# A four-layer graph network on one core: first node states interleaved by four, segment flags moved into the first attention pass, edge parts one supertile earlier

## The chip, the core and the metric

The kernel runs on one core of one Trainium2 chip. A core has five engines with a queue of instructions each: TensorE (PE in the profile, its weight loads PEld), VectorE (DVE), ScalarE (ACT), GpSimd (POOL) and SyncE (SP), and 16 DMA engines. [...] SP only issues DMAs here; GpSimd issues the indirect ones (gathers and scatters). The metric is the device time of one execution in microseconds (us).

## The reference

The graph has 5000 nodes and 80000 edges, sorted by destination; node states and edge attributes have 128 features. Four layers follow each other, each on the normalised and rectified state, each added back to it:

```python
h = relu(layernorm(x)); x = x + L0(h, edges, edge_attr_128)   # three steps of attention (GAT) + GRU
h = relu(layernorm(x)); x = x + L1(h, edges)                  # GIN: a sum of neighbours, two matmuls, batch norm
h = relu(layernorm(x)); x = x + L2(h, edges, edge_attr_4)     # four steps of a gated graph network
h = relu(layernorm(x)); x = x + L3(h, edges)                  # graph transformer
```

Layer 0, the one of the change, computes in each of its three steps, with H = 4 heads of 32:

```python
q = x[dst] @ wq.T + bq
k = (x[src] + edge_attr) @ wk.T + bk          # v likewise
a = softmax over the edges of one dst of sum(q * k, per head) / sqrt(32)
out[dst] = sum over its edges of a * v
```

followed by a projection, layer norms, a two-layer MLP and a GRU cell on the nodes. The part `edge_attr @ wk.T` (and wv) is the same in all three steps.

## The kernel before, in words

**Tiling.** Nodes are held transposed, features on the 128 partitions, in 10 groups (`NG`) of 512 columns (`GW`); the last group is partly empty. Edges are cut into 157 supertiles (`NSUP`) of four tiles of 128 edges. Because the edges are sorted, the destinations of a supertile lie in a window of 128 nodes that moves by 32 a supertile.

**Order of the work.** The Tile layer allocates the buffers, sets the semaphores and orders the instructions of each engine; inside `tc.manual_schedule()` the order is that of the program text. Around the change:

1. `tile_gnn` (L1844) loads the destinations and checks that the sorted form fits; `sorted_graph` (L782) then loads small weights and constants.
2. `index_edges` (L869 to 912) loads sources and the four edge type scores, finds each edge's type on DVE, transposes the indices on TensorE into `srcx`, `typx`, `dneg`, and stores two tables, `key_t` (L905, L909) and `dl_t` (L912), through SP.
3. The weights of layer 0 are loaded (L1532, 1.18 MB). Then come the *first states* (L1536 to 1562): for each group the rows of x are loaded (L1549, through SP, two buffers), transposed (L1555), copied from PSUM (L1557), stored, normalised and rectified by `Chain.norm` (L1063 to 1092), and turned into rows of k, v, q by `qkv_tables` (L1127 to 1141), which stores them in the tables `kv_t` and `q_t`. `norm` is a chain: matmul L1066 (centre), Square on ACT L1069, four small matmuls L1074 (variance), Sqrt L1077, reciprocal and a diagonal on DVE L1079 and L1080, matmul L1083 (spread over partitions), copy L1085, product L1088. `qkv_tables` is four times a matmul L1132 and an addition on DVE L1135. Generators write these chains: each `yield` ends a step. Here `alone()` runs a chain to its end before the next group begins.
4. `segments` (L914 to 925) makes, for each of the 20 chunks (`NCH`) of eight supertiles, flags that tell where a destination's run of edges begins and ends. Per chunk: one load of destinations, two DVE instructions, one store into `seg_t`, with two buffers.
5. `gat_pass` (L1265 to 1410) runs three times, in manual order. One loop step `s` does the following, in this order: two zero blocks of the count table for later layers (`zero_counts`, first pass only, 120 in all); a step of `place_counts` (first pass only), which ends in 185 scatters on GpSimd; `prefetch(s + 4)`: in the first pass the raw edges `e` (L1281), then the query rows `qw` and destinations `dl`, all from SP, and four gathers of kv rows by GpSimd (L865); the sums of supertile `s - 12` (L1206); the addition of the edge part to the gathered kv (L1377, DVE); `edge_part(s + 1)` (first pass); products with the queries (L1383) and the values with their edge part (L1385); `expand(s + 1)`, which spreads the queries over the edges on TensorE (L1247); the scores (L1391); `flip_edges(s + 2)` (first pass); the weighted values (L1260) and the one-hot of supertile `s - 11` (`one_hot`, L1212 to 1220, five ACT instructions); `flip(s + 2)` for the queries (L1240, DVE). Between these, four calls of `go()` each advance one step of a softmax chain and of a node chain (`gat_node`).

`flip_edges` transposes the raw edges on TensorE (L1297) and copies them on ACT (L1299). `edge_part` multiplies them with the weights of k and v (L1308), copies the result on ACT (L1310) into `ekv` and stores it (L1311) for passes two and three, which load it instead. Each lives in a dictionary under its supertile's number:

```python
            if here:
                n, kv, e = tiles_of(s), kvs.pop(s), ekvs.pop(s)
                V.tensor_add(kv[:, :n, :D], kv[:, :n, :D], e[:, :n, :D])
            if first and 0 <= s + 1 < NSUP:
                edge_part(s + 1)
```

Of the kernel before, what the change touches and what calls it, by code (L numbers as in the profile page):

```python
# [47 lines left out]
P = 128  # L48
# [3 lines left out]
G = 4  # L52
# [702 lines left out]
def tiles_of(s):  # L755
    return min(G, NT - s * G)
# [25 lines left out]
def sorted_graph(ctx: ExitStack, tc, x, src, ea, ea4, wpack, rpack, out, dpad, dnat):  # L782
# [86 lines left out]
    def index_edges():  # L869
        with tc.tile_pool(name="ix", bufs=1) as ix, \  # L870
                tc.tile_pool(name="ip", bufs=2, space=PSUM) as ip:
            n = NT // TI
            src_i = ix.tile([n, TI * P], I32, name="src_i")
            Y.dma_start(src_i, src.rearrange("(p c) -> p c", p=n))
            e4 = ix.tile([n, TI * P, 4], F32, name="e4")
            Y.dma_start(e4, ea4.rearrange("(p c) f -> p c f", p=n))
            top = ix.tile([n, TI * P], F32, name="top")

            V.tensor_reduce(top, e4, axis=AX.X, op=OP.max)
            V.tensor_tensor(e4, e4, top[:, :, None].to_broadcast([n, TI * P, 4]), op=OP.is_equal)  # L880
# [28 lines left out]
            Y.dma_start(key_t[E:].rearrange("(a b) -> a b", b=P), none)  # L909
            dlb = ix.tile([n, TI * P], BF16, name="dlb")  # L910
            V.tensor_copy(dlb, dnat)
            Y.dma_start(dl_t.rearrange("(p c) -> p c", p=n), dlb)  # L912

    def segments():  # L914
        with tc.tile_pool(name="iw", bufs=2) as iw:


            for c in range(NCH):
                d = iw.tile([P, 258], I32, name="d")
                at = dpad.offset + FRONT + c * CH * G * P - 65  # L920
                Y.dma_start(d, bass.AP(tensor=dpad.tensor, offset=at, ap=[[P, CH * G], [0, 4], [1, 258]]))
                sg = iw.tile([P, 2, 257], BF16, name="sg")
                V.tensor_tensor(sg[:, 1, :], d[:, 1:], d[:, :257], op=OP.is_equal)
                V.tensor_scalar(sg[:, 0, :], sg[:, 1, :], BIG, -BIG, op0=OP.mult, op1=OP.add)
                Y.dma_start(seg_t[c * P:(c + 1) * P, :], sg.rearrange("p a f -> p (a f)"))

    class Banks:

# [333 lines left out]
                     w[:, :, None].to_broadcast([P, n * heads, D // heads]))  # L1262
        return pv

    def gat_pass(ew, ps, sc, kv_tab, q_tab, first, node, place=None):  # L1265
# [10 lines left out]

        def prefetch(s):
            n = tiles_of(s)
            if first:
                e = raws[s] = ew.tile([P, G, D], F32, name="e", bufs=AHEAD + 1)  # L1280
                Y.dma_start(e[:, :n], ea[s * SUP:s * SUP + n * P, :].rearrange("(t p) f -> p t f", p=P))  # L1281
            else:
# [72 lines left out]

        scatters, blocks = [], list(range((NG - GD) * ROWSB)) if place else []

        for s in range(-AHEAD, NSUP + LAG + 1):
            here, late, sum_ = 0 <= s < NSUP, s - LAG, s - LAG - 1
            for i in blocks[:2]:  # L1360
                zero_counts(i)
# [13 lines left out]
            if here:  # L1375
                n, kv, e = tiles_of(s), kvs.pop(s), ekvs.pop(s)
                V.tensor_add(kv[:, :n, :D], kv[:, :n, :D], e[:, :n, :D])  # L1377
# [11 lines left out]
            if here:  # L1389
# [132 lines left out]
    def alone(chain):  # L1522
        for _ in chain:
            pass


    index_edges()


    with ExitStack() as st:  # L1530
        w0 = st.enter_context(tc.tile_pool(name="w0", bufs=1))
        load_weights(w0, "0")  # L1532
        q0 = W("0_qkv", 256, P)
        V.tensor_scalar_mul(q0, q0, 1.0 / math.sqrt(32.0))

        with tc.tile_pool(name="xw", bufs=2) as xw, tc.tile_pool(name="xb", bufs=8, space=PSUM) as xb:  # L1536
# [4 lines left out]
            for g in range(NG):  # L1541
                gr = Group(xw, xb, g, 2)
                ch = Chain(gr)
                xr = xw.tile([P, BPG, D], F32, name="xr")
                n = min(GW, N - g * GW)
                full = n // P
                if n < GW:
                    V.memset(xr, 0.0)
                Y.dma_start(xr[:, :full, :],  # L1549
                            x[g * GW:g * GW + full * P, :].rearrange("(t p) f -> p t f", p=P))  # L1550
                if n > full * P:
                    Y.dma_start(xr[:n - full * P, full, :], x[g * GW + full * P:g * GW + n, :])
                p = ch.bank()
                for i in range(BPG):
                    T.transpose(p[:, i * P:(i + 1) * P], xr[:, i, :], ident)  # L1555
                xt = gr("y")
                S.copy(xt, p)  # L1557
                Y.dma_start(ch.rows(st_x), xt)
                a = gr("ha")
                alone(ch.norm(a, xt, 1e-5, relu=True))  # L1560
                Y.dma_start(ch.rows(st_a), a)
                alone(ch.qkv_tables(a, "0_qkv", True, kv_t[0], q_t[0]))
# [48 lines left out]
        for step in range(3):  # L1611
            def node(g, sums, step=step):
                gr = Group(nw, ps, g)
                gr.load("ha", st_a, 2)
                gr.load("hb", st_h if step else st_a, 2)
                return chains(gat_node, gr, sums, step, tags=("bank", "flat"))

            with ExitStack() as once:
                place = None
                if step == 0:  # L1620
                    pw = once.enter_context(tc.tile_pool(name="pw", bufs=1))
                    place = place_counts(pw, lambda: ps.tile([P, GW], F32, name="flat"))
                with tc.manual_schedule():
                    gat_pass(ew, ps, sc, kv_t[step % 2], q_t[step % 2], step == 0, node, place)


    with ExitStack() as st:
# [321 lines left out]
```

## Time and profile before

| What | us |
|---|---|
| Median of 3 timed runs | 9317.53 |
| Lowest and highest | 9316.03, 9318.48 |
| Profiled execution, own time | 7963.37 |
| Its span, first to last instruction | 7961.3 |
| TensorE busy | 6558.0 (82%) |
| VectorE, ScalarE, GpSimd busy | 3409.5, 3475.0, 4893.2 |
| Mean granted TensorE clock | 0.866 |
| First states in the span | 65 to 205 |
| Segment flags | 209 to 254 |
| First attention pass | 254 to about 1700 |

The profile is of one execution, which took less time than the timed ones. Its page lists the busy time of each engine, then the span in 40 equal slices with one digit for each (tenths of the slice in which the engine was busy, or of the full clock that TensorE was granted). Groups of instructions carry the line of the source, the engine, and `out<-in` by tile names. The chain of work that ended last is followed back from the end: at each step to what released the instruction. The list of waits says which engine's instruction stood idle, for whom, for how many us in total, how often, and the longest of them.

### The profile page before, as it was taken

To read this page: it belongs to the slowest core of one execution; us is meant where nothing else is said; L and a number is where in the kernel's file an instruction comes from. 1 tells how busy PE (TensorE), PEld (TensorE's weight loads), DVE (VectorE), ACT (ScalarE), POOL (GpSimd) and SP (SyncE) were. 2 spreads that over 40 slices of the span, in tenths; PEclk is the share of its full clock that TensorE was granted. 3 is DMA by queue.
4 is the path that set the end of the run, shared out by engine and by line. 5 is a ranking of instruction groups with operands and counts; after the bars stand their busy time and mean duration, and the time that the engine had idled before them with its cause. 6 is when DMAs were issued, how large, how long until landed. Compare 5 with 4: busy or idle time off the path is not lost.

```text
span 7961.3 us, 95797 instructions
## 1 busy us (share of the span) xinstructions
PE 6558.0 (82%) x32485; PEld 4429.3 (56%) x32485; DVE 3409.5 (43%) x6132; ACT 3475.0 (44%) x8112; POOL 4893.2 (61%) x4978
## 2 busy tenths in 40 slices
PE   4577777766888757777799999999999999989888
PEld 2456556545666546666545555555555555556554
DVE  3566554547777657777500121111111110135555
ACT  1254554543444424544433434444444445544433
POOL 0444777417666357666177647767767767767774
PEclk8788988976777767777799999999999999988888
DMA  3898566637666556666266576666666666645553
GB/s 108 302 315 254 174 184 175 183 98 234 217 217 215 158 168 220 217 210 218 83 197 185 164 243 220 210 197 219 204 199 223 203 202 217 208 138 141 142 141 100
DMA packets 852101, 1532.96 MB, mean 193 GB/s; under 512 B 137518, under 2 KB 513177, under 8 KB 851335
## 3 DMA queue, kind: packets, MB, share of 16 engines
q1 hardware_dynamic: 652724, 1049.27, 40.4%
q0 software_dynamic: 198880, 477.47, 21.0%
q8 instruction: 263, 4.31, 0.2%
q14 instruction: 234, 1.92, 0.1%
HBM read 1240.53 MB, written 285.99 MB: 192 GB/s over the span
## 4 chain that ended last, share of the span: by engine, by line
PE 64%; ACT 9%; DMA 8%; DVE 8%; issue 6%; POOL 5%; SPq 0%; DVEq 0%; POOLq 0%; ACTq 0%
PE acc L1206 17%; PE dense L1752 11%; PE each L1247 7%; DMA m<-tr_t,typx 4%; PE flat L1308 4%; PE dense L1675 4%; PE bank L1060 3%; POOL m L865 3%; ACT oh L1218 3%; PE den L1206 3%; PE bank L1083 2%; PE bank L1099 2%; ACT oh L1219 2%; PE bank L1100 1%; POOL kv L865 1%
## 5 line engine op out<-in xcount | busy, mean ns | idle before, releaser
L865 POOL DMA_INDIRECT kv<-kv_t,srcx x2500 | 2524.9, 1010 | 1814.2 <-issue 658.3
L865 POOL DMA_INDIRECT m<-tr_t,typx x1824 | 1743.3, 956 | 731.5 <-issue 444.9
L1218 ACT ACTIVATE oh<-iota_row,dneg 128x128 f32<-128x128 f32 x4780 | 1524.2, 390 | 1474.4 <-PE acc L1206 1331.1
L1206 PE MATMUL acc<-oh,pv 128*128 128x128 f32 (+4 forms) x6152 | 1178.6, 336 | 427.4 <-ACT oh L1219 341.3
L1206 PEld LDWEIGHTS acc<-oh,pv 128*128 128x128 f32 x6152 | 1023.1, 242 | 764.2 <-ACT oh L1219 465.3
L1752 PE MATMUL dense<-counts,terms_in 128*128 128x512 bf16 (+1 forms) x5760 | 1264.4, 372 | 0.0
L1247 PE MATMUL each<-qw,oht 128*128 128x128 f32 x5000 | 883.2, 333 | 365.3 <-issue 185.1
L1247 PEld LDWEIGHTS each<-qw,oht 128*128 128x128 f32 x5000 | 806.3, 240 | 501.0 <-issue 252.7
L1206 PEld LDWEIGHTS acc<-oh,m 128*128 128x128 f32 x5520 | 732.2, 196 | 329.4 <-DMA m<-tr_t,typx 152.0
L1752 PEld LDWEIGHTS <-terms_in 128*128 128x128 bf16 x5760 | 578.2, 101 | 591.9 <-issue 101.8
L1206 PE MATMUL acc<-oh,m 128*128 128x128 f32 (+4 forms) x5520 | 783.9, 283 | 147.3 <-DMA m<-tr_t,typx 132.4
L1219 ACT ACTIVATE oh<-oh 128x512 f32<-128x512 f32 (+1 forms) x1198 | 752.9, 628 | 37.7
L1108 DVE SCALAR_TENSOR_TENSOR gate<-bank,wt_s,gate 128x512 f32<-128x512 f32 x70 | 50.7, 724 | 1487.3 <-PE bank L1060 1487.3
L865 POOL DMA_INDIRECT m<-h_t,srcx x456 | 431.0, 945 | 302.7 <-DVE gate L1162 164.1
L1377 DVE TENSOR_TENSOR kv<-kv,ekv 128x512 f32<-128x512 f32 x471 | 320.6, 681 | 211.1 <-ACT ekv L1310 116.6
L1310 ACT COPY ekv<-flat 128x512 f32<-128x512 f32 x313 | 183.3, 586 | 504.4 <-PE flat L1308 489.1
L1308 PE MATMUL flat<-wt,et 128*128 128x256 f32 x1250 | 389.5, 467 | 9.1 <-ACT et L1299 9.1
L1383 DVE TENSOR_TENSOR qk<-kv,each 128x512 f32<-128x512 f32 x471 | 321.1, 682 | 84.3 <-PE each L1247 55.8
L1240 DVE TENSOR_SCALAR oht<-dl,pcol 128x512 f32<-128x512 bf16 (+1 forms) x628 | 307.9, 490 | 39.4 <-DMA dl<-dl_t 37.7
L1385 DVE TENSOR_TENSOR v<-kv,ekv 128x512 f32<-128x512 f32 x471 | 320.7, 681 | 0.0
L1260 DVE TENSOR_TENSOR pv<-v,sm_w 128x512 f32<-128x512 f32 x471 | 318.9, 678 | 0.0
L1391 DVE TENSOR_REDUCE sc<-qk 128x16 f32<-128x512 f32 x471 | 317.6, 674 | 0.0
(321 smaller groups left out, 7157.7 us busy)
## 6 DMA issues: line engine op xcount, KB each, us to landing
counts<-count_t SPq DMA_DIRECT2D x600, 512.0 KB
ekv<-ekv_t SPq DMA_DIRECT2D x312, 512.0 KB
dl<-dl_t SPq DMA_DIRECT2D x624, 128.0 KB
ekv_t<-ekv SPq DMA_DIRECT2D x156, 512.0 KB
count_t<-zero_b SPq DMA_DIRECT2D x120, 512.0 KB
terms_in<-split_t SPq DMA_DIRECT2D x150, 384.0 KB
qw<-q_t SPq DMA_DIRECT2D x628, 64.0 KB
kv<-kv_t,srcx POOLq DMA_INDIRECT x2500
```

Of the source, the lines that this page charges most:

```text
L865: Q.indirect_dma_start(out=to, out_offset=None, in_=table, in_offset=bass.IndirectOffsetOnAxis(ap=idx, axis=0), **kw)
L1206: T.matmul(self.bank(g)[:, at:at + hi - lo], lhsT=values, rhs=oh[:, lo:hi], start=False, stop=s == last_of_group(g) and t == tiles_of(s) - 1)
L1218: S.activation(oh[:, t, :], iota_row, AF.Abs, bias=dneg[:, k:k + 1])
L1219: S.activation(oh[:, :n], oh[:, :n], AF.Relu, scale=-1.0, bias=1.0)
L1247: T.matmul(p[:, t, :], lhsT=oht[:, t * P:(t + 1) * P], rhs=qw, start=True, stop=True)
L1260: V.tensor_mul(pv[:, :n].rearrange("p t (h w) -> p (t h) w", h=heads), v[:, :n].rearrange("p t (h w) -> p t h w", h=heads), w[:, :, None]. ...
L1308: T.matmul(p[:, i, :], lhsT=et[:, t + i, :], rhs=W("0_qkv", 0, 256), start=True, stop=True)
L1377: V.tensor_add(kv[:, :n, :D], kv[:, :n, :D], e[:, :n, :D])
L1383: V.tensor_mul(qk[:, :n], kv[:, :n, :D], pqs.pop(s)[:, :n])
L1385: V.tensor_add(vs[s][:, :n], kv[:, :n, D:], e[:, :n, D:])
L1675: T.matmul(p[:, :w], lhsT=terms[:, k, :], rhs=counts[:, t, :w], start=False, stop=last and k == 2 and t == 3)
L1752: T.matmul(dense[g][t][:, :w], lhsT=terms[:, k, :], rhs=counts[:, t, :w], start=False, stop=last and k == 2)
```

## The change

Five edits are made together.

- `index_edges()` is called after the weights of layer 0 are loaded, and its three stores go out on GpSimd's queue in place of SP's.
- The first states are written as a generator, `first_state`. All ten groups' rows of x are loaded at the start, into ten buffers, by DMAs on ScalarE's queue. Then four chains are under way at a time, advanced in turn by one step each, in manual order; each chain has two PSUM banks of its own, and a new one is begun when one ends.
- `segments` becomes a generator of three steps a chunk (load; two DVE instructions; store). One step is taken in each loop step of the first attention pass.
- The loop of `gat_pass` begins at `s = -6` in place of -4. The raw edges are loaded by `load_edges(s + 6)`, apart from the rest of `prefetch(s + 4)`.
- `edge_part` and `flip_edges` are called for one supertile further ahead.

```diff
-            Y.dma_start(key_t[:E].rearrange("(p c) -> p c", p=n), srcf)
+            Q.dma_start(key_t[:E].rearrange("(p c) -> p c", p=n), srcf)
...
-            Y.dma_start(dl_t.rearrange("(p c) -> p c", p=n), dlb)
-
-    def segments():
-        with tc.tile_pool(name="iw", bufs=2) as iw:
...
+            Q.dma_start(dl_t.rearrange("(p c) -> p c", p=n), dlb)
+
+    def segments(iw):
...
+        for c in range(NCH):
+            d = iw.tile([P, 258], I32, name="sg_d", bufs=2)
+            at = dpad.offset + FRONT + c * CH * G * P - 65
+            Y.dma_start(d, bass.AP(tensor=dpad.tensor, offset=at, ap=[[P, CH * G], [0, 4], [1, 258]]))
+            yield
+            sg = iw.tile([P, 2, 257], BF16, name="sg_f", bufs=2)
+            V.tensor_tensor(sg[:, 1, :], d[:, 1:], d[:, :257], op=OP.is_equal)
+            V.tensor_scalar(sg[:, 0, :], sg[:, 1, :], BIG, -BIG, op0=OP.mult, op1=OP.add)
+            yield
+            Y.dma_start(seg_t[c * P:(c + 1) * P, :], sg.rearrange("p a f -> p (a f)"))
+            yield
...
-        H, AHEAD, LAG = 4, 4, CH + 3
+        H, AHEAD, FAR, LAG = 4, 4, 6, CH + 3
...
+        def load_edges(s):
+            n = tiles_of(s)
+            e = raws[s] = ew.tile([P, G, D], F32, name="e", bufs=FAR - 1)
+            Y.dma_start(e[:, :n], ea[s * SUP:s * SUP + n * P, :].rearrange("(t p) f -> p t f", p=P))
...
-        for s in range(-AHEAD, NSUP + LAG + 1):
+        for s in range(-FAR, NSUP + LAG + 1):
...
+                next(flags, 0)
+            if first and 0 <= s + FAR < NSUP:
+                load_edges(s + FAR)
...
-            if first and 0 <= s + 1 < NSUP:
-                edge_part(s + 1)
+            if first and 0 <= s + 2 < NSUP:
+                edge_part(s + 2)
...
-            if first and 0 <= s + 2 < NSUP:
-                flip_edges(s + 2)
+            if first and 0 <= s + 3 < NSUP:
+                flip_edges(s + 3)
...
-    index_edges()
...
         load_weights(w0, "0")
+        index_edges()
...
+        def first_state(ch, xr):
+            p = ch.bank()
+            for i in range(BPG):
+                T.transpose(p[:, i * P:(i + 1) * P], xr[:, i, :], ident)
+            yield
+            xt = ch.t("y")
+            S.copy(xt, p)
+            yield
+            Y.dma_start(ch.rows(st_x), xt)
+            a = ch.t("ha")
+            yield from ch.norm(a, xt, 1e-5, relu=True)
+            Y.dma_start(ch.rows(st_a), a)
+            yield from ch.qkv_tables(a, "0_qkv", True, kv_t[0], q_t[0])
+
+        AT_ONCE = 4
+        with tc.tile_pool(name="xw", bufs=AT_ONCE) as xw, tc.tile_pool(name="xb", bufs=1, space=PSUM) as xb:
+            xb = Banks(xb, **{f"bank{i}": 2 for i in range(AT_ONCE)})
+            todo = []
+            for g in range(NG):
+                xr = xw.tile([P, BPG, D], F32, name="xr", bufs=NG)
...
+                S.dma_start(xr[:, :full, :],
+                            x[g * GW:g * GW + full * P, :].rearrange("(t p) f -> p t f", p=P))
...
+                todo.append(first_state(Chain(Group(xw, xb, g, AT_ONCE), tag=f"bank{g % AT_ONCE}"), xr))
...
+            with tc.manual_schedule():
+                under_way = []
+                while todo or under_way:
+                    while todo and len(under_way) < AT_ONCE:
+                        under_way.append(todo.pop(0))
+                    under_way = [c for c in under_way if next(c, xw) is not xw]
-        segments()
...
+                    flags = segments(pw)
```

More of the change, by code (lines that the diff above doesn't have):

```diff
@@ L908, in index_edges @@
             V.memset(none, -1.0)
-            Y.dma_start(key_t[E:].rearrange("(a b) -> a b", b=P), none)
+            Q.dma_start(key_t[E:].rearrange("(a b) -> a b", b=P), none)
             dlb = ix.tile([n, TI * P], BF16, name="dlb")
             V.tensor_copy(dlb, dnat)
-            Y.dma_start(dl_t.rearrange("(p c) -> p c", p=n), dlb)
-    def segments():
-        with tc.tile_pool(name="iw", bufs=2) as iw:
[L918 to L925, printed above, removed]
+            Q.dma_start(dl_t.rearrange("(p c) -> p c", p=n), dlb)
[11 more added lines that the diff above has]
+            yield
     class Banks:
@@ L1263, in weigh, with gat_pass @@
         return pv
-    def gat_pass(ew, ps, sc, kv_tab, q_tab, first, node, place=None):
-        H, AHEAD, LAG = 4, 4, CH + 3
+    def gat_pass(ew, ps, sc, kv_tab, q_tab, first, node, place=None, flags=None):
+        H, AHEAD, FAR, LAG = 4, 4, 6, CH + 3
         sums, qs = Sums(ps), Queries(ew, ps, q_tab, AHEAD)
@@ L1278, in prefetch @@
             n = tiles_of(s)
[L1279 to L1282, printed above, removed]
+            if not first:
                 e = ekvs[s] = ew.tile([P, G, 256], F32, name="ekv", bufs=AHEAD + 1)
@@ L1532, in sorted_graph @@
         load_weights(w0, "0")
+        index_edges()
         q0 = W("0_qkv", 256, P)
         V.tensor_scalar_mul(q0, q0, 1.0 / math.sqrt(32.0))
-        with tc.tile_pool(name="xw", bufs=2) as xw, tc.tile_pool(name="xb", bufs=8, space=PSUM) as xb:
+        def first_state(ch, xr):
[17 more added lines that the diff above has]
+                xr = xw.tile([P, BPG, D], F32, name="xr", bufs=NG)
+                n = min(GW, N - g * GW)
+                full = n // P
+                if n < GW:
+                    V.memset(xr, 0.0)
+                S.dma_start(xr[:, :full, :],
+                            x[g * GW:g * GW + full * P, :].rearrange("(t p) f -> p t f", p=P))
+                if n > full * P:
+                    S.dma_start(xr[:n - full * P, full, :], x[g * GW + full * P:g * GW + n, :])
+                todo.append(first_state(Chain(Group(xw, xb, g, AT_ONCE), tag=f"bank{g % AT_ONCE}"), xr))
             no_rows = xw.tile([ROWS0, D], F32, name="no_rows", bufs=1)
@@ L1540, in sorted_graph @@
                 Y.dma_start(q[:ROWS0, :], no_rows)
[L1541 to L1562, printed above, removed]
-        segments()
+            with tc.manual_schedule():
[4 more added lines that the diff above has]
+                    under_way = [c for c in under_way if next(c, xw) is not xw]
         ew = st.enter_context(tc.tile_pool(name="ew0", bufs=1))
@@ L1618, in sorted_graph @@
             with ExitStack() as once:
-                place = None
+                place = flags = None
                 if step == 0:
@@ L1622, in sorted_graph @@
                     place = place_counts(pw, lambda: ps.tile([P, GW], F32, name="flat"))
+                    flags = segments(pw)
                 with tc.manual_schedule():
-                    gat_pass(ew, ps, sc, kv_t[step % 2], q_t[step % 2], step == 0, node, place)
+                    gat_pass(ew, ps, sc, kv_t[step % 2], q_t[step % 2], step == 0, node, place, flags)
     with ExitStack() as st:
```

## The prediction

> **What bounds the kernel now.** I read the page first: its span, and the slices for a poorly used stretch.
>
> ```profile
> span 7961.3 us, 95797 instructions
> PE   4577777766888757777799999999999999989888
> PEclk8788988976777767777799999999999999988888
> ```
>
> One digit is 199 us. TensorE is busy everywhere except in the first two slices, where the changed code lies. I placed the stages by the timeline: indexing of the edges until 58, first states from 65.0 (the first transpose) to 205.2, segment flags from 208.9 to 254, first GAT pass from 254 to about 1700. The windows of these stages (columns: window, its length, then busy time and count of PE, PEld, DVE, ACT, POOL, then granted clock, DMA share, GB/s):
>
> ```profile
> 65.00:205.00 140.00, 96.06 (x240) 48.69 (x240) 40.57 (x77) 22.90 (x42) 0.00 (x0) 0.76 0.31 104
> 205.00:254.00 49.00, 0.00 (x0) 0.00 (x0) 13.38 (x41) 0.00 (x0) 0.00 (x0) 0.52 0.44 124
> 258.00:480.00 222.00, 151.29 (x777) 126.37 (x775) 149.42 (x292) 87.87 (x187) 140.47 (x139) 0.85 1.06 373
> 480.00:1640.00 1160.00, 881.24 (x4448) 691.65 (x4449) 663.09 (x1210) 598.07 (x1234) 676.07 (x672) 0.89 0.66 201
> ```
>
> Row 2 is the flags: TensorE, ScalarE and GpSimd do nothing for 49 us. Row 3, the first 30 or so supertiles of the pass, is bound by DMA (share 1.06). Row 4 is not. Then the chain that ended last, in the window of the first states, and in the one of the flags:
>
> ```profile
> by line: PE bank L1132 36.5%; PE bank L1083 11.1%; PE bank L1074 8.9%; PE bank L1066 8.8%; DVE ln_s L1080 5.0%; DVE ha L1088 5.0%; ACT ln_s L1069 4.3%; ACT y L1557 4.2%; ACT ln_s L1085 4.2%; PE bank L1555 3.8%; issue 3.5%; DMA xr<-in_x 3.3%
> by line: DMA seg_t<-sg 51.8%; DMA d<-dpad 11.2%; DVE sg L923 8.3%; DMA q_t<-qkv_rows 5.9%; SPq L921 5.3%; DVE sg L924 4.6%; issue 3.6%; SPq L1281 3.0%; SPq L940 2.2%; SPq L1233 1.5%; SPq L925 1.3%; DVE qkv_rows L1135 1.1%; SPq L1231 0.9%; S
> ```
>
> In the first states the chain hops PE, ACT, PE, DVE, PE inside one group: groups run one after another, 13.5 us each ((190.0 - 82.0) / 8, starts of their transposes). In the flags it is 20 store latencies behind two buffers. For the pass, one round of the chain:
>
> ```profile
> 1065.93 0.89 PE acc L1206 x8
> 1066.83 1.77 PE flat L1308 x8
> 1068.60 0.89 PE each L1247 x8
> 1069.49 0.45 PE flat L1297 x4
> 1069.94 0.02 issue
> 1069.96 0.59 ACT et L1299
> 1070.55 1.18 ACT oh L1218 x4
> 1071.73 0.02 issue
> 1071.75 0.64 ACT oh L1219
> 1072.39 0.04 issue
> ```
>
> This is a ring: L1206 (sums) waits for the one-hot, which stands on ScalarE behind the copy of the flipped edges L1299, which waits for the flip L1297, which stands on TensorE behind L1247, L1308 and the sums of the step before. DVE isn't in it. What TensorE and DVE wait for in the pass:
>
> ```profile
> PE acc L1206 <- ACT oh L1219: 196.6, 101, 4.1
> DVE kv L1377 <- ACT ekv L1310: 114.3, 31, 7.8
> ```
>
> **What the Trainium skill says.** "TensorE: Matmul & The Clock Gate", Part 1: the array runs at half clock until it has been busy for some 3.4 us, and falls back after an idle window. The trace agrees in kind: L1066 takes 2.08 us for group 0 and 1.12 for group 1, the first states are granted 0.76, the idle flags 0.52. Part 1 also gives ScalarE and VectorE strict first-in first-out queues; in each round above L1218 starts as L1299 ends. "Trainium Kernel Development and Optimization", Key Constraints: DMAs of the SP, ACT and POOL queues share the same 16 engines, so another queue saves issue time only. The trace before has no load on ACT's queue to test that.
>
> **The change part by part.** All sums are against the profiled execution (span 7961.3, own time 7963.4). The timed runs' median is 9317.5, 1354 more; the profile does not show where that lies, and I carry savings over one to one.
>
> *1. Indexing after the weights; x on ACT's queue; three stores on POOL's.* The weights (1.18 MB, 5.2 us on the wire before: 58.4 to 63.6) now go ahead of the edge types, whose landing starts the chain of the indexing (DMA 15.4 us, then DVE 37.1 to 53.3). A delay of 0 to 4 us there. Then the 11 x loads no longer stand behind key_t's store, the weights and the zero rows (59.7), but on ACT. They still wait for the pool of the indexing to be free; the key store took 4.7 us from SP, and from POOL it is not shown: one indirect DMA there occupies it 1.0 us, so I add 0 to 2. Gain 0 to 3 from the shorter queue. Net -4 to +3; I take a loss of 2. x loaded at once is by itself worth nothing: TensorE waited for x once (11.9 us, at the start), because two buffers hid the rest. Eleven issues at 0.4 us on ACT come before its first copy, while it would wait for x anyway (66.2 us of idle before).
>
> *2. Four groups at a time.* No work is removed: TensorE, DVE and ACT were busy 9.6, 4.1 and 2.3 us per group of 13.5. Interleaved, each engine's next instruction belongs to another group, so TensorE's own work is the bound. At full clock, from the pass's own chain rows: transposes 0.45, L1066 0.86, L1074 0.95, L1083 0.86, L1132 4 x 0.65 = 2.6: 5.7 us. The longest reply hidden is L1074 to L1083 (0.26 on ACT, 0.18 + 0.69 on DVE, some 1.5 with waits), against 3 x 0.95 of the other three groups: covered. In the qkv rounds DVE needs 4 x 0.6 = 2.4 against 2.6. Banks (two a group) come free one round earlier. Ten groups are 4 + 4 + 2. At the 0.89 the pass gets, a group costs 6.4: eight cost 51; the last pair exposes its latency, 11.5 (one group at full clock) + 3 = 15; filling and the x loads (four at 256 KB before the round closes) 4. Sum 70, so 140 - 70 = **70 saved**. Ends: 5.7 x 8 + 14 = 60 (80 saved); the old pace of 9.6 kept, 77 + 18 = 95 (45 saved). The 40 stores, about 0.5 us each on SP, are 20 us within 70.
>
> *3. Flags into the pass.* Before, 254.1 - 205.6 = 48.5 us lie between the last table store and the pass's first load; what must remain is that store's landing, 3.1. **45 saved.** Added to the pass, one part a step over 60 steps: 20 x (0.43 + 0.23) = 13 us of DVE, hidden by its 43% idle; 40 issues at 0.55 = 22 us of SP, hidden since SP stood waiting 600 us for ScalarE's ekv; 20 x (132 + 131) KB. Some ten of those chunks fall into the DMA-bound stretch: 2.6 MB at 373 GB/s = **7 us lost**; without that cover lost for all twenty, 14. The flags are ready at step 3c - 4, loaded at 8c + 4: never late. Queued behind the compare on DVE is the kv add of the step, and SP's flag store has the prefetches behind it: see the last rival.
>
> *4. Loop from -6.* Two more opening steps put up to four zero blocks and two edge loads ahead of the first gathers' partners qw and dl on SP: +5 us of prologue (before: 254.1 to 266.5), but these 2 MB then no longer ride in the DMA-bound stretch (-5). Zero; -3 to +3. In passes two and three these steps are empty.
>
> *5. Edge parts one further ahead.* Same instructions and same order on TensorE and ScalarE (L1206, L1308, L1247, L1297; L1310 twice, L1299, L1218, L1219), so the ring keeps its period. What goes is the 114 us in which DVE waits for ekv, which is idle time off the chain. Only where TensorE waits for DVE's qk (11 us before 480, 3 after) or a softmax on DVE (13 us) can it return something. 0 to 25; I take 0. Edges are loaded three steps before their flip, not two: TensorE waited 14 us for them, all before 480, where the DMA rate binds; 0. Nor can the ring run much faster between 822 and 1391: GpSimd issues gathers and scatters there without a break (7 x 1.27 = 8.9 us a step against 9.1).
>
> Sum: 70 + 45 - 2 - 7 = **106 saved**: span about 7855, time 9317.5 - 106 = **9211.5**.
>
> **Rivals.** *A, the forecast*, 9190 to 9235. *B, the interleaving is not dense*: TensorE keeps its half-warm pace or SP's stores stall the tiles, the first states take 95 to 105: 45 + 45 - 11 = 79 or less, 9238 to 9250. For it: the clock of 0.76, though that stage is full of gaps; against: in the pass at 76% busy it gets 0.89. *C, the edge lead does matter*: DVE running free shortens the steps with softmax and node chains, +25 and the full-clock first states +10: 9175. Against it: the ring. *D, slower*: place: the flag compare at the head of a step on DVE. It waits for a load issued one step before; in the DMA-bound stretch edge loads took 8.4 to 10.7 us against a step of 7.2, so a compare is 3.5 late in a third of the steps, with kv, qk, oht and TensorE's L1247 behind it. Over ten chunks that is 35 us, less DVE's slack (2.9 a step), and the gain stays. It ends slower only if each of the 20 chunks costs the ring over (106 + 19) / 20 = 6.2 us, which needs the late load in the unsaturated part too. In that case about 9340. *E, the timed runs grant another clock*: if the 1354 us were TensorE at 0.8 of its pace, both sides of part 2 stretch and the saving grows by some 10.
>
> **How the numbers follow.** A 0.62 (with E inside), B 0.18, C 0.12, D slower 0.04, gains cancelled to no change 0.04. A difference under 0.2% (19 us) can't be told from none here. The range reaches from C with E (-151: 9166) to B at its worst end (45 + 44 - 4 - 14 - 10 = 61: 9257): 9166 to 9258. Faster 0.92, same 0.04, slower 0.04.
>
> **What would show it.** The first states last 60 to 80 us with a clock near 0.9 and TensorE over 85% busy; no flag store ahead of the pass; the pass's first load near 140; steps up to s = 30 still at share 1.05; from there 9.1 us a step as before; DVE's wait for ekv gone and the wait of L1206 for the one-hot unchanged at some 200 us. I am wrong if the pass changes length by over 25 us, or if the first states stay above 95.

## The result, and the profile after

The changed kernel takes 9179.25 us (median of 4 runs, 9174.76 to 9188.83) and the kernel before 9317.17 us: a ratio of 0.9853 (95% interval 0.9836 to 0.987), so 138 us are saved where 106 were forecast (9211.5). The time of either kernel goes with the chip: in these runs and in the last experiment the kernel before takes about 9310 us, on the three chips of the other experiments about 7960, as in the profile of before (own time 7963.37). So the two pages shown first, before's and after's, can't be laid over each other. The changed kernel was therefore run again (label f_after), and that run fell on a chip of the quicker kind: 7863.42 us (7861.08 to 7872.77) against 7965.64, a ratio of 0.9873 (0.9857 to 0.989), 102 us saved (88 to 114 by the interval). Three values had been put down ahead of it: 97 us if the parts measured one by one add up, 106 if the forecast's sum holds there, 138 if the saving is the same everywhere. The 138 is out; the interval holds both others. The trace of f_after answers to the one on which the forecast was built.

From the page of the changed kernel in the 9174.76 us run, and then from the page of f_after, the rows that were shown of before:

```profile
span 9172.9 us, 95718 instructions
...
PE   5676667747777477777988788788788788867878
...
PEclk8897888857777677777998898898899899878777
```

```profile
span 7863.9 us, 95493 instructions
...
PE   5677777757788757777899999989899899978888
...
PEclk8898889867777867777799999999999999988988
```

One slice is 229 us in the first page and 197 in the second. In the second the pass begins within the first slice (at 140 us), and TensorE opens with 5 and 6 tenths where it was 4 and 5. The stages of f_after, in the columns of the stage table of before: first states; the gap to the pass; the pass from the issue of its first edge load to the scores of step 30 (the start of the 31st L1398); the rest of the pass up to its last scores.

```profile
61.77:136.33 74.56, 69.38 (x240) 40.62 (x240) 41.30 (x83) 22.10 (x42) 0.00 (x0) 0.91 0.58 191
136.33:140.82 4.49, 0.00 (x0) 0.00 (x0) 0.00 (x0) 0.00 (x0) 0.00 (x0) 0.68 0.81 265
140.82:406.48 265.66, 168.02 (x847) 140.61 (x850) 162.20 (x324) 95.10 (x202) 145.30 (x144) 0.82 1.04 355
406.48:1554.70 1148.22, 864.83 (x4380) 678.26 (x4387) 659.61 (x1214) 593.15 (x1228) 675.28 (x668) 0.90 0.65 199
```

And the last two of these of the kernel before:

```profile
254.14:494.83 240.69, 164.25 (x831) 136.88 (x832) 156.57 (x302) 92.69 (x197) 146.52 (x144) 0.84 1.05 365
494.83:1641.70 1146.87, 869.60 (x4400) 682.25 (x4398) 658.83 (x1204) 594.45 (x1228) 672.36 (x668) 0.90 0.66 199
```

The first states, from the first transposes to the last table store, fell from 140.6 us (65.06 to 205.65) to 74.6, the gap from 48.5 (205.6 to 254.1) to 4.5. TensorE's work in the first states, 96 us before, fell to 69; its clock rose from 0.76 to 0.91, which alone would give 80. The clock is not the whole of it: 24 of the 27 us are in the qkv matmuls (L1132, 815 ns each in the mean; now L1134, 489), while those of L1066 and L1083 take as long as before (12.2 and 15.4 us; now 12.1 and 15.0). The stretch to step 30 grew from 240.7 to 265.7 us, at nearly the same DMA share (1.05 and 1.04) but at 355 GB/s in place of 365. The rest is unchanged (1146.9 and 1148.2). The bookkeeping between these two traces: the pass's first edge load is issued 113.3 us earlier, 25.0 are given back by step 30 and 1.4 by the end of the pass, and what follows the pass is 10.4 us shorter (6319.6 to 6309.2), though nothing was changed there. 113.3 - 25.0 - 1.4 + 10.4 = 97.3, which is the difference of the spans (97.4) but for rounding. Two other traces of the kernel before have 6309.8 and 6318.8 us after the pass, so those 10 us are what differs from one execution to the next.

The chain that ended last, in the first states of f_after (66 to 137 us):

```profile
by line: PE bank L1134 34.9%; PE bank L1085 20.7%; PE bank L1068 16.8%; PE bank L1076 12.4%; DMA q_t<-qkv_rows 6.0%; PE bank L1545 3.1%; issue 2.5%; SPq L1142 2.0%; ACT y L1548 1.7%; DVE ha L1090 1.0%; DVE ln_s L1082 1.0%; ACT ln_s L1087 0.
```

Four TensorE lines make 85% of it, the qkv matmuls first; the ScalarE and VectorE steps, which stood at 4 to 5% each before, are at 1 to 2%. One round of the chain in the pass, which before was the ring of L1206, L1308, L1247, L1297, L1299, L1218, L1219 (now L1208, L1312, L1249, L1301, L1303, L1220, L1221):

```profile
1016.02 0.89 PE each L1249 x8
1016.91 0.45 PE flat L1301 x4
1017.36 0.02 issue
1017.38 0.58 ACT et L1303
1017.97 1.18 ACT oh L1220 x4
1019.15 0.02 issue
1019.17 0.64 ACT oh L1221
1019.81 0.04 issue
1019.86 1.16 PE acc L1208 x8
1021.01 1.74 PE flat L1312 x8
```

Apart from L1208 (1.16 us, 0.89 before) the durations are those of before. What the engines wait for in the pass (130 to 1650 us; total, times, longest):

```profile
PE acc L1208 <- ACT oh L1221: 234.7, 117, 4.1
...
DVE sg_f L923 <- DMA sg_d<-dpad: 68.0, 8, 17.0
```

The wait for the one-hot is as it was (238.8 us, 117 times, over the pass in e_before, another trace of the kernel before). VectorE's wait for ekv is gone from the list. In its place stands a new one, 68.0 us for the input (`sg_d`) of the flags.

### The profile page after: what moved, and what is told of

Read it like the earlier page. It is cut to its first block, busy times and chain, and to the rows that moved or that the text cites. A ratio compares the mean times of both kernels' runs of the same rounds, so it can differ in the third digit from the quotient of the medians.

```text
span 9172.9 us, 95718 instructions
## 1 busy us (share of the span) xinstructions
PE 6933.8 (76%) x32485; PEld 4605.3 (50%) x32485; DVE 3396.2 (37%) x6132; ACT 3465.2 (38%) x8112; POOL 4853.0 (53%) x4981
## 5 line engine op out<-in xcount | busy, mean ns | idle before, releaser
L865 POOL DMA_INDIRECT kv<-kv_t,srcx x2500 | 2486.0, 994 | 2328.8 <-DVE v L1392 978.6
L1220 ACT ACTIVATE oh<-iota_row,dneg 128x128 f32<-128x128 f32 x4780 | 1523.5, 390 | 2410.7 <-PE acc L1208 1074.3
L1208 PE MATMUL acc<-oh,pv 128*128 128x128 f32 (+4 forms) x6152 | 1240.9, 348 | 562.9 <-ACT oh L1221 254.2
L1208 PEld LDWEIGHTS acc<-oh,pv 128*128 128x128 f32 x6152 | 1077.0, 253 | 920.8 <-issue 520.2
L1770 PE MATMUL dense<-counts,terms_in 128*128 128x512 bf16 (+1 forms) x5760 | 1381.5, 389 | 199.3 <-issue 184.9
L1249 PE MATMUL each<-qw,oht 128*128 128x128 f32 x5000 | 926.3, 344 | 580.3 <-issue 322.5
L1249 PEld LDWEIGHTS each<-qw,oht 128*128 128x128 f32 x5000 | 844.4, 250 | 723.4 <-issue 416.5
L1208 PE MATMUL acc<-oh,m 128*128 128x128 f32 (+4 forms) x5520 | 818.2, 290 | 199.9 <-issue 172.7
L1208 PEld LDWEIGHTS acc<-oh,m 128*128 128x128 f32 x5520 | 771.4, 206 | 386.0 <-issue 299.4
L1221 ACT ACTIVATE oh<-oh 128x512 f32<-128x512 f32 (+1 forms) x1198 | 753.0, 629 | 37.8
L1312 PE MATMUL flat<-wt,et 128*128 128x256 f32 x1250 | 409.8, 487 | 30.9 <-ACT et L1303 27.6
L1693 PE MATMUL dense<-counts,terms_in 128*128 128x512 bf16 (+1 forms) x1440 | 340.5, 385 | 35.2 <-issue 34.2
L1312 PEld LDWEIGHTS flat<-wt,et 128*128 128x128 f32 x1250 | 302.0, 254 | 85.8 <-ACT et L1303 30.7
```

Source lines behind the costliest of these rows:

```text
L865: Q.indirect_dma_start(out=to, out_offset=None, in_=table, in_offset=bass.IndirectOffsetOnAxis(ap=idx, axis=0), **kw)
L1208: T.matmul(self.bank(g)[:, at:at + hi - lo], lhsT=values, rhs=oh[:, lo:hi], start=False, stop=s == last_of_group(g) and t == tiles_of(s) - 1)
L1220: S.activation(oh[:, t, :], iota_row, AF.Abs, bias=dneg[:, k:k + 1])
L1221: S.activation(oh[:, :n], oh[:, :n], AF.Relu, scale=-1.0, bias=1.0)
L1249: T.matmul(p[:, t, :], lhsT=oht[:, t * P:(t + 1) * P], rhs=qw, start=True, stop=True)
L1312: T.matmul(p[:, i, :], lhsT=et[:, t + i, :], rhs=W("0_qkv", 0, 256), start=True, stop=True)
```

## The experiments

All were run against the kernel before on the same chip. "To step 30" is the length from the issue of the pass's first edge load to the scores of step 30, in the one trace of the run; the MB are those of all DMA packets in it.

| label | what it is | time | saved against before (ratio, interval) | to step 30 | MB |
|---|---|---|---|---|---|
| (before) | medians; three traces | 7953 to 7968 | | 238.4 to 241.0 | 87.8 to 88.1 |
| e_states_alone | first states and indexing only | 7894.3 | 74 (0.991, 0.9896-0.9923) | 237.6 | 88.1 |
| e_flags_first | changed, flags ahead of the pass | 7891.0 | 77 (0.99, 0.9886-0.9914) | 244.8 | 91.1 |
| e_no_lead | changed, edge parts one ahead | 7874.6 | 94 (0.9882, 0.9867-0.9897) | 264.9 | 93.7 |
| f_after | the changed kernel | 7863.4 | 102 (0.9873, 0.9857-0.989) | 265.7 | 94.3 |
| f_flags_ahead | flag input a chunk earlier | 7851.6 | 114 (0.9855, 0.9839-0.9872) | 255.8 | 94.4 |
| f_opening | other order at the opening | 7848.1 | 118 (0.9854, 0.9837-0.987) | 256.2 | 88.7 |
| f_both | both edits | 7843.9 | 122 (0.9851, 0.9835-0.9867) | 240.3 | 88.7 |
| g_no_lead | f_both, edge parts one ahead | 7838.5 | 115 (0.9853, 0.9837-0.987) | 237.9 | 88.2 |
| g_near_loads | f_both, loop from -4 | 7842.8 | 110 (0.986, 0.9844-0.9877) | 248.1 | 88.4 |

**The kernel before again (e_before, g_before).** No edit.

> The kernel before again, unchanged, to have a trace of an execution that takes about 9317 us, as the timed ones do; the profile of before lies in one of 7963 us. If the 1354 us between them are spread over the whole kernel, each 100 us of the pass does about 1.17 times less than in that profile, and the first states take about 160 us in place of 140. If they lie in stages other than the first states and the first pass, both stages look as they did.

> The kernel before once more, for a second trace of it on this chip. If it takes about 7966 us, its first pass from the first load to step 30 takes 240 to 243 us as in the traces so far. If it takes about 9317 us, its trace beside that of the changed kernel (span 9172.9) shows in which stage the 36 us lie that the change gains there over the 102 gained here: in the first pass, in the stages before it, or in the passes after it, which the change doesn't touch.

They took 7949.37 and 7968.55 us, so the question of the 1354 us was answered another way: by the one kernel of which there are traces from both kinds of chip, the changed one. On the chip of 9179 us against f_after, the stages are: to the pass's first edge load 137.1 and 140.8 us; to step 30, 283.2 and 265.7; the rest of the pass 1318.8 and 1148.2; after it 7433.8 and 6309.2. The stages ahead of the pass take about the same time on both, the stretch to step 30 is 1.07 times longer, and what follows is 1.15 to 1.18 times longer. It shows as a lower clock (0.817, 0.871 over the span) and as TensorE standing still with nothing shown to wait for. In the waits of the whole span, first of the run of 9174.76 us, then of f_after:

```profile
PE each L1249 <- issue: 322.5, 115, 18.9
...
PE acc L1208 <- issue: 298.3, 324, 6.1
```

```profile
PE each L1249 <- issue: 188.8, 83, 6.8
...
PE acc L1208 <- issue: 4.8, 22, 0.2
```

"Issue" ahead of L1208, 298.3 us in 324 times there, is 4.8 in 22 here. No trace of the kernel before comes from the slower chip, so the stage in which it loses the 36 us more than elsewhere (138 - 102) could not be read.

**The first states alone (e_states_alone).** The flags go back to a loop of their own ahead of the pass, and the edge lines back to where they were:

```diff
-        H, AHEAD, FAR, LAG = 4, 4, 6, CH + 3
+        H, AHEAD, FAR, LAG = 4, 4, 4, CH + 3
...
-                next(flags, 0)
...
-            if first and 0 <= s + 2 < NSUP:
-                edge_part(s + 2)
+            if first and 0 <= s + 1 < NSUP:
+                edge_part(s + 1)
...
-            if first and 0 <= s + 3 < NSUP:
-                flip_edges(s + 3)
+            if first and 0 <= s + 2 < NSUP:
+                flip_edges(s + 2)
...
+        with tc.tile_pool(name="iw", bufs=2) as iw:
+            alone(segments(iw))
...
```

> The kernel before with only the indexing, its queues and the first states as changed (four groups at a time, inputs loaded at once); flags ahead of the pass, edge loads and edge parts where they were. Forecast: 70 us of first states less and 2 us of indexing more, 9249. If the first states are where the gain beyond the forecast comes from: 9215 to 9225. If they give only the 38 to 45 us of the less dense rival: 9270 to 9280.

74 us saved (61 to 83 by the interval). In the trace the pass's first edge load comes 63.9 us earlier than in the profile of before, and the stretch to step 30 is as before. The less dense rival (38 to 45 us) is out, and on this kind of chip the first states give about what was forecast (68). Where the 138 us of the slower kind come from this run can't tell, since it did not fall on such a chip.

**The flags back ahead of the pass (e_flags_first).** Only the flags are undone:

```diff
-                next(flags, 0)
...
+        with tc.tile_pool(name="iw", bufs=2) as iw:
+            alone(segments(iw))
...
```

> The changed kernel with the flags made ahead of the pass, as before; everything else stays. Forecast: 45 us of gap come back and 7 us of DMA time go from the stretch that DMA bounds, so 9217, and the pass's first load 45 us later. Rival (the flags in the pass hold up VectorE at its opening or beyond): 9195 or less, the pass gives back 20 us or more of the gap. Rival (the flags cost the pass nothing, or the gap had grown): 9225 to 9230.

The flags in the pass are worth 25 us (102 - 77), read from two chips; on the chip of e_flags_first itself, e_no_lead, which is the changed kernel but for the lead, gives 16 (94 - 77). Either is less than the forecast's 38: of the 45 us of gap the pass gives back 20 to 29, as the first rival has it. The stretch to step 30 shows two losses apart. From e_states_alone to e_flags_first come the loop from -6 and the lead, without flags; from there to f_after the flags. The windows of the first two kernels to step 30:

```profile
190.27:427.84 237.57, 157.52 (x825) 131.73 (x828) 157.55 (x302) 92.79 (x197) 147.67 (x144) 0.86 1.05 371
```

```profile
190.40:435.23 244.83, 166.98 (x845) 139.29 (x848) 156.64 (x302) 94.93 (x201) 146.53 (x144) 0.83 1.06 372
```

The loop from -6 costs 7.3 us in this stretch: 3.0 MB more, at 372 GB/s 8.1 us. In the time of the whole kernel no loss shows (7891.0 us against the 7894.3 of e_states_alone, on the same chip). The flags add 20.8 us more: 3.2 MB (94.3 - 91.1), 8.6 us at 372 GB/s, and the rest because the rate falls from 372 to 355 GB/s (94.3 MB would have taken 253 us; they took 265.7).

**The flags' input a chunk earlier (f_flags_ahead).** If the rate falls because VectorE stands behind a late compare, an earlier load must bring it back, with the same bytes:

```diff
-        for c in range(NCH):
+        def load(c):
             d = iw.tile([P, 258], I32, name="sg_d", bufs=2)
...
+            return d
+
+        new = load(0)
+        yield
+        for c in range(NCH):
+            d = new
+            if c + 1 < NCH:
+                new = load(c + 1)
```

> The changed kernel with the input of each flag chunk loaded one chunk earlier (four steps ahead of its compare, not one). Theory 1 (the late compare holds up the steps): VectorE's wait for it falls from some 60 us to under 15, and 8 to 15 us are won. Theory 2 (the rate of the DMA engines binds there, the wait only shows it): the wait goes to another place and the time stays within 4 us of the changed kernel.

```profile
138.66:394.50 255.84, 158.51 (x838) 130.98 (x841) 163.72 (x325) 94.45 (x200) 143.69 (x144) 0.87 1.06 369
...
DVE oht L1250 <- DMA dl<-dl_t: 65.6, 23, 11.8
```

12 us faster than f_after on the same chip (7847.55 to 7853.07 against 7861.08 to 7872.77), at 94.4 MB and 369 GB/s: 9.8 us less to step 30. The wait for the flag input is gone from the list of waits of the pass. Almost as much went elsewhere, as theory 2 said: VectorE's `oht`, the one-hot that spreads the queries, waits 65.6 us for dl, in 23 times (2.6 us in f_after). But the time falls by what theory 1 gave and not by theory 2's 4 us at most: that the input was late did cost 10 to 12 us. Why the wait for dl does not cost the same is open.

**Another order at the opening (f_opening).** The opening of the pass in f_after: on SP the first issue of dl and that of the second chunk's flag input (the first chunk's went out at 59.9 us), then VectorE up to the first kv add (start, time taken, and in brackets the idle time before and what ended it).

```profile
149.41 1.14 SPq L1235 DMA_DIRECT2D dl<-dl_t  x1
...
151.84 1.32 SPq L920 DMA_DIRECT2D sg_d<-dpad  x1
...
160.75 0.43 DVE L923 TENSOR_TENSOR sg_f<-sg_d 128x257 bf16<-128x257 int32 x1 [17.02 <-DMA sg_d<-dpad]
...
161.36 0.48 DVE L1242 TENSOR_SCALAR oht<-dl,pcol 128x512 f32<-128x512 bf16 x1
...
164.44 0.69 DVE L1384 TENSOR_TENSOR kv<-kv,ekv 128x512 f32<-128x512 f32 x1
```

The first dl is issued 8.6 us after the first edge load (140.82), behind four zero blocks, two more edge loads and a flag store. The flag input issued at 151.84 lands 8.9 us later, the compare L923 waits for it until 160.75, and the one-hot L1242 of step 0, for which L1249 on TensorE waits, starts behind it. The compare is not what makes the opening late, though: in f_flags_ahead, where it waits for nothing, the first kv add comes 22.5 us after the first edge load, and here 23.6. The edit puts the prefetch first, and zero blocks and flags from step 0 on:

```diff
-            for i in blocks[:2]:
-                zero_counts(i)
-            blocks = blocks[2:]
+            if 0 <= s + AHEAD < NSUP:
+                prefetch(s + AHEAD)
+            if s >= 0:
+                for i in blocks[:2]:
+                    zero_counts(i)
+                blocks = blocks[2:]
...
-                next(flags, 0)
+                if s >= 0:
+                    next(flags, 0)
```

> The changed kernel with another order of loads at the opening of the pass: queries and destinations of a step ahead of everything else, zero blocks and flags only from step 0. Theory 1 (the opening is late because qw and dl stand behind zero blocks, edge loads and flags on SP): the first kv add comes 12 to 14 us after the pass's first load, not 23, and about 10 us are won. Theory 2 (the DMA engines are full there in any order): what is put off comes back in the stretch that DMA binds, and at most 3 us are won.

```profile
138.84:395.02 256.18, 167.50 (x837) 141.09 (x840) 162.20 (x322) 94.46 (x200) 146.18 (x144) 0.82 1.02 346
```

15 us faster, where theory 1 had about 10 and theory 2 at most 3. The first kv add comes 10.9 us after the first edge load, not 23.6. Of these 12.7 us, 9.5 are left by step 30: there are 88.7 MB instead of 94.3, since zero blocks (0.5 MB each, two a step) and flags start six steps later, yet the rate is down to 346 GB/s, with the compare still late (52.8 us in 11 waits). So the opening was not the whole of it. The edit changes both the order on SP and the bytes ahead of the first dl; which of the two made the opening late it doesn't tell.

**Both edits (f_both).** The two diffs above together.

> The two edits before this together. If both theories 1 hold: 18 to 25 us faster than the changed kernel. If both theories 2 hold: within 5 us of it.

```profile
142.05:382.36 240.31, 160.77 (x838) 135.43 (x841) 163.16 (x322) 94.38 (x200) 144.60 (x144) 0.85 1.06 369
```

19.5 us faster than the changed kernel, within what theory 1 expected, but less than the two gains one by one (11.8 and 15.4); against f_opening alone it is 4 us, inside the spread of the runs. In the trace the stretch to step 30 is back at the 240 us of before, with the flags in it: 88.7 MB at 369 GB/s. All its runs (7837.26 to 7853.53 us) lie below all those of the changed kernel and of the kernel before on that chip. What was put off is written after step 30, where the DMA share of f_after is 0.65, and no cost shows there: from step 30 to the pass's end f_both takes 1134.0 us, f_after 1148.2, the three traces of before 1140.7 to 1153.7.

**The edge parts (e_no_lead, g_no_lead).** In both, one ahead in place of two, once in the changed kernel and once in f_both:

```diff
-            if first and 0 <= s + 2 < NSUP:
-                edge_part(s + 2)
+            if first and 0 <= s + 1 < NSUP:
+                edge_part(s + 1)
...
-            if first and 0 <= s + 3 < NSUP:
-                flip_edges(s + 3)
+            if first and 0 <= s + 2 < NSUP:
+                flip_edges(s + 2)
```

> The changed kernel with the edge parts back where they were, one supertile ahead and the flip two ahead; the earlier loads, the flags in the pass and the first states stay. Forecast: DVE's wait for the edge parts comes back (above 100 us in some 30 times), the time stays within 15 us of the changed kernel's 9179. Rival (the lead is worth something): 9205 to 9215, 25 to 35 us slower than the changed kernel.

> The kernel with both edits (flag input a chunk earlier; queries and destinations first, zero blocks and flags from step 0) with the edge parts back to one supertile ahead. Forecast (the lead lies off the ring): VectorE's wait for the edge parts is back at 90 to 110 us, the time within 6 us of the kernel with both edits (7844, ratio 0.9851). Rival (once VectorE is no longer held up by flags, the lead pays): 10 us or more slower.

The ratio moves from 0.9873 to 0.9882 in the first pair and from 0.9851 to 0.9853 in the second, far inside the intervals. VectorE's wait for the edge parts comes back in both, 98.9 us in 27 times in e_no_lead and here in g_no_lead, over the pass:

```profile
DVE kv L1394 <- ACT ekv L1322: 91.4, 24, 7.7
```

91.4 us of waiting, in 24 times, whose cost does not show in the time: the lead rival (25 to 35 us) is out.

**The edge inputs four ahead again (g_near_loads).**

```diff
-        H, AHEAD, FAR, LAG = 4, 4, 6, CH + 3
+        H, AHEAD, FAR, LAG = 4, 4, 4, CH + 3
...
```

> The kernel with both edits with the edge inputs loaded four supertiles ahead and the loop from -4, as in the kernel before; the edge parts stay two ahead. If the two more opening steps only push back the opening: 4 to 8 us faster than the kernel with both edits, and the first kv add comes 12 us after the pass's first load. If TensorE waits for edge inputs loaded one step before their flip: slower by 3 to 10 us, with a wait of L1301 for e.

```profile
142.79:390.85 248.06, 163.89 (x849) 138.11 (x850) 162.81 (x328) 95.10 (x202) 145.17 (x144) 0.86 1.03 356
...
PE flat L1309 <- DMA e<-in_edge_attr: 17.5, 8, 4.1
```

Not the 4 to 8 us of the first theory: 110 us saved against 122 (and 115 in g_no_lead, on the same chip as this run), the intervals overlap, and no gain shows. Nor is the opening shorter: the first kv add comes 11.4 us after the first edge load, 11.3 in f_both. TensorE now waits 17.5 us for e (2.5 in f_both), and the stretch to step 30 is 8 us longer than in f_both, at 356 GB/s. So in this stretch the earlier loads help once what they displaced is out of the way; that the whole kernel gains by them is not shown.

**Two groups at a time (h_two_at_once).** `AT_ONCE = 2` in the changed kernel.

> The changed kernel with two groups at a time in the first states, not four. By the forecast's own term for a pair (15 us: 11.5 for one group at full clock and 3 for what the second adds) five pairs and 4 us of filling take 79 us, so 8 us more than four at a time (71 measured), with TensorE's clock still above 0.85. Rival (with two groups each reply is exposed, TensorE's clock falls towards the 0.76 of one at a time): 95 us or more, 24 us slower.

This run fell on a chip of the slower kind: 9186.7 us (9180.5 to 9205.5), 0.9871 (0.9853 to 0.9889) of before, an interval that overlaps the changed kernel's. Its trace against that of the 9174.76 us run is sharper: the pass's first edge load comes 8.1 us later (145.3, 137.1), as the term for a pair said, with the granted clock at 0.98 in the first states (0.93 with four at a time):

```profile
62.00:140.00 78.00, 66.01 (x240) 36.39 (x240) 43.14 (x85) 22.40 (x42) 0.00 (x0) 0.98 0.54 180
```

The rival (the clock falls towards 0.76 with two groups) is out: a second group is enough to keep the clock up, and the third and fourth together are worth 8 us more.

## Why the prediction was right, and where it was not

The sign and the range held, and on the quicker kind of chip, that of the profile, the sum did too: 106 forecast, 102 measured (88 to 114). Point by point:

1. *Indexing and queues*: -2 forecast. The first transposes start at 61.77, not 65.06, 3.3 us earlier: x arrives 3.4 us after its first issue (58.37), where it took 5.4, probably since the weights are gone from the wire. But the step "eleven issues at 0.4 us on ACT come before its first copy, while it would wait for x anyway" failed: nine issues take 7.38 us, 0.8 each, and the table load and the first copy stand behind them (next fence). The copy starts at 67.12, before at 67.51: the 0.4 us that are left are less than the three traces of before differ by (67.19 to 68.06).

```profile
58.37 7.38 ACTq L1566 DMA_DIRECT2D xr<-in_x  x9
65.83 1.28 ACT L1548 ACT_TABLE_LOAD   x1 [65.83 <-DVE same L960]
67.12 0.58 ACT L1548 COPY y<-bank 128x512 f32<-128x512 f32 x1
```

2. *First states*: 70 forecast, 74.6 in f_after and 70.3 in the 9174.76 us run (62.30 to 132.63); with point 1, 69.3 us saved where 68 were forecast. TensorE was busy 93% of it (69.4 of 74.6) at a clock of 0.91; over 85% and about 0.9 were forecast. A group cost it 6.9 us, not 6.4. The half clock of an idle array, which the Trainium skill states ("TensorE: Matmul & The Clock Gate", Part 1), agrees in kind: the gap between the stages is granted 0.68.
3. *Flags*: 45 forecast for the gap, 44.0 measured. The store's landing that had to remain took 4.2 us (3.1). The bytes cost 8.6 us where 7 were forecast. What failed is "13 us of DVE, hidden by its 43% idle": the work was hidden, the wait for its input was not. It was put into rival D, with a price of 3.5 us in a third of the steps, and left out of the sum. The run shows 68.0 us of waiting in 8 times, up to 17.0, of which 10 to 12 reach the time. The threshold for a slower kernel (6.2 us a chunk over twenty chunks) was far off.
4. *Loop from -6*: zero forecast; 7.3 us are lost by step 30 in the traces, though the whole time shows no loss (e_flags_first against e_states_alone). The step that failed there is the credit: "these 2 MB then no longer ride in the DMA-bound stretch (-5)". The opening is itself bound by the DMA engines as soon as more is put there: from the first edge load to the first kv add the share rises from 0.88 (e_states_alone) to 1.01 (e_flags_first), and the add comes after 21.4 us in place of 12.6. The bytes (2.6 MB for four zero blocks and two edge loads; 3.0 MB more in the traces) were not moved out of the stretch but into its beginning, and what stands behind them came later.
5. *Edge parts further ahead*: 0 forecast, nothing measurable in two pairs of runs. The ring was read rightly.

The pass grew by 26.3 us from its first edge load to its last scores (1387.6 to 1413.9; by 19 and 35 against the other two traces of before). In two of these three comparisons that is past the mark of 25 at which the text calls itself wrong: for the pass it was wrong. So the point forecast owes part of its accuracy to luck: the pass lost 19 us more than forecast (26.3, not 7), and against that stand the 10 us after the pass, which are chance in these two traces.

The step by which 9211.5 missed 9179.25 is another one: "I carry savings over one to one". On the slower chip the same change saves 138 us (121 to 153 by the interval). Rival E had the direction, with 10 us. A scaling by the ratio of the times would give 102 x 1.17 = 119, and 103 to 133 with the interval of the 102, so a plain scaling isn't excluded; one to one is. Since the stages ahead of the pass take about the same time on both chips in the changed kernel, scaling the first states is not it, unless the kernel before is slower there; that is open, as no trace of it on such a chip exists. That 9175 of rival C lies nearest is chance: its mechanism, the lead, was measured at nothing.

## What to carry to other kernels

A small piece of work slipped into a busy loop is hidden only if its input is there when the engine's queue comes to it: issue its load several steps ahead, not one. Here, in a DMA-bound stretch, compares of 0.43 us held VectorE for 68 us in all, and loading their input four steps ahead won 12 us of the time. Work that only has to be done some time (here 120 stores of 0.5 MB of zeros) is best put where the DMA engines have room; ahead of a DMA-bound stretch it delays the first inputs, and its bytes are not free there either. A wait that is off the ring need not be removed: here 91 us of it made no difference that shows.

## What the runs showed of the hardware

- The same kernel takes 7863 or 9179 us, and each chip on record shows only one of the two. The stages ahead of the first pass take about the same time on both (140.8 and 137.1 us); those from step 30 on are 1.15 to 1.18 times longer, with a clock of 0.817 against 0.871 and TensorE standing still for no shown reason (ahead of L1208 alone 298.3 us against 4.8). Of the engines only TensorE is busy longer (6933.8 us against 6499.3; VectorE 3396.2 and 3406.2, ScalarE 3465.2 and 3472.4, GpSimd 4853.0 and 4895.1). In the clock records of the two traces the time granted full clock is the same (5751 and 5762 us); the time at half clock is 3357 us against 2031, which is all of the difference. What holds TensorE there is open.
- In the DMA-bound stretch the busy share of the DMA engines goes from 1.06 to only 1.02 where the rate falls from 369 to 346 GB/s (f_both, f_opening): the GB/s show the fall more plainly than the share.
- Issuing DMAs is not free to ScalarE: nine loads of 256 KB took 7.38 us of it, 0.8 each in the mean; the shortest of the ten took 0.37 (f_after).
